# Another order of the features in the recurrent stage: 512-byte runs for x's second load and the output's stores

## The chip, the cores and the metric

The kernel runs on one core of a Trainium2 chip, as one program. The metric is device time in microseconds (us). Before the change three runs took 1760.66, 1766.8 and 1768.66 us; their median is 1766.8 us. A further execution was taken with the hardware profiler, and took 1754.42 us. All arrays are float32.

## The reference

The input x has 16 batches (B) of 256 time steps (T) with 512 features (D); cond has 16 rows of 512. Two layers follow one another, each added to its input:

```python
# layer 0: attention, its norm scaled and shifted by cond
scale, shift = jnp.split(cond[:, None] @ W_emb + b_emb, 2, axis=-1)
xn = _rms_norm(x, g_norm) * (1.0 + scale) + shift
q, k, v = ...            # xn @ W_qkv, split into 16 heads of 32 features
q, k = _rms_norm(q, g_q), _rms_norm(k, g_k)
attn = softmax(q @ k.T * 32 ** -0.5)
o = attn @ v             # heads joined again to 512 features
x = x + o + o @ W_out

# layer 1: a GRU over the 256 steps, started from h = cond
def cell(h, x):
    i_r, i_z, i_n = jnp.split(x @ W_ih + b_ih, 3, axis=-1)
    h_r, h_z, h_n = jnp.split(h @ W_hh + b_hh, 3, axis=-1)
    r = sigmoid(i_r + h_r); z = sigmoid(i_z + h_z)
    n = tanh(i_n + r * h_n)
    return (1.0 - z) * n + z * h
x = x + scan(cell, cond, x over time)
```

## The kernel before

The core has these engines: TensorE (matmuls, PE in the profile, with its weight loads as PEld), VectorE (DVE), ScalarE (ACT), GpSimd (POOL) and SyncE (SP), which here only issues DMAs. P is 128, the number of partitions; KC is 4, the number of 128-wide pieces of the 512 features.

**Opening and attention.** Batch by batch, load_x brings a batch of x into SBUF with time on the partitions. The norm's statistics are taken on ScalarE (norm_first, L171), the rows are scaled on VectorE (norm_apply, L178), turned by TensorE so that features lie on the partitions (turn_x, L194), then scaled and shifted by cond (put_x). project (L220) multiplies by W_qkv; four matmuls with 32 columns of weights each fill the four 32-column strips of the array. Logits, maxima, exponentials, normalization and the weighted sum follow in four slots per batch (slot0 to slot3), each slot overlapping the attention of one group of heads with the projection of the next batch. The result stays in SBUF as oT, features on partitions. In the opening, batches 0, 1 and 2 go through the first steps with nothing yet to overlap: `load_x(0)`, `load_x(1)`, `load_x(2)` stand among the loads of the weights in SP's queue.

**Recurrent stage.** State, inputs and outputs lie with features on the partitions, 32 features of one "q" of each 128-wide piece per 32-partition strip. x is loaded a second time for it, in blocks of 8 steps (TG), by load_block (L687): eight DMAs of 32 KB per block, one for each strip j and half of the block s. in_blocks gives the access pattern in DRAM. put_block (L733) turns a block on VectorE in 32 x 32 squares. output_step (L719) and put_output add the attention's output projection to it, a group of 16 steps ahead of use. For a step, the gates r, z and n are accumulated in PSUM: the bias (open_gate, L757, for the first two pairs of steps; seed, L769 to L771, after that), the input's part for two steps at once (input_part) and the state's part (state_part), both through gate_part (L775), which puts the state or input on the array as weights of 16 or 32 columns and streams 128 columns of wih or whh past it, once for each of the four strips. VectorE turns the gates in 32 x 32 squares (L799), ScalarE applies sigmoid and tanh, VectorE updates h, and GpSimd adds x (L908). After 8 steps store (L811) turns the block back on VectorE and writes it in eight DMAs of 32 KB. The last block is turned by TensorE and written by store_last.

Which feature sits in which strip is set in four places that have to agree: in_blocks, the columns that gate_part streams, the columns of wo that product and project_first use, and the rows of wih and whh, which must match the features on the partitions. The bias rows b_rows are made from two row loads (L118, L119), a transpose (L628), and in slot2 of batches 1 to 4 a broadcast copy and a 32 x 32 transpose for each row of gates (L476, L479).

**What sets the order.** TensorE, VectorE, ScalarE and GpSimd run their instructions in the order in which the program text issues them. DMAs go to SP's queue (and a few to ScalarE's) in the order of the text, each one waiting for its inputs or for its buffer. A completion semaphore is given to each DMA in turn out of eight, so a DMA also waits until the one eight places before it has landed.

Of the kernel before, what the change touches and what calls it, by code (L numbers as in the profile page):

```python
# [8 lines left out]
F32 = mybir.dt.float32  # L9
# [10 lines left out]
def kernel(  # L20
# [52 lines left out]
    for k in range(KC):  # L73
        nc.scalar.dma_start(cond_sb[k * B : (k + 1) * B, :], cond[:, k * P : (k + 1) * P])
    h0T = const.tile([P, KC, B], F32, name="h0T")

    cols = const.tile([P, 38], F32, name="cols")

# [24 lines left out]

    rows_b = p1.tile([26, P], F32, tag="qkn", name="rows_b", bufs=4)

    wq = wpool.tile([P, KC, 3 * D], F32, tag="w_b", name="wq")
    for i in range(3):
        for k in range(KC):
            nc.sync.dma_start(
                wq[:, k, i * D : (i + 1) * D], w_qkv[k * P : (k + 1) * P, i * D : (i + 1) * D]  # L110
            )
        if i == 0:
            for r, g in ((0, g_q), (1, g_k)):
                nc.sync.dma_start(
                    rows_b[r : r + 1, :].rearrange("o (i d) -> o i d", d=DH),
                    g.rearrange("(o i d) -> o i d", o=1, i=1).to_broadcast([1, HG, DH]),
                )
            nc.sync.dma_start(rows_b[2:14, :], b_ih.rearrange("(m c) -> m c", c=P))  # L118
            nc.sync.dma_start(rows_b[14:26, :], b_hh.rearrange("(m c) -> m c", c=P))  # L119
        if i == 1:  # L120
            load_x(1)


# [3 lines left out]
    qT = p1.tile([P, NG, T], F32, name="qT")  # L127
    kT = p1.tile([P, NG, T], F32, name="kT")


# [316 lines left out]
    def slot2(b, w, prev, st):  # L447
# [19 lines left out]
        if b == 0:  # L467

            for c in range(KC):
                d = wo[:, c, c * P : (c + 1) * P]  # L470
                nc.vector.tensor_tensor(d, d, ident, ALU.add)
        elif b <= 4:
            i = b - 1
            wide = small.tile([P, KC, 32], F32, tag="wide", name=f"wide_{i}", bufs=1)
            c0 = (0, 4, 8, 20)[i]
            nc.vector.tensor_copy(  # L476
                wide, cols[:, 14 + c0 : 18 + c0].unsqueeze(2).to_broadcast([P, KC, 32])
            )
            nc.vector.transpose(b_rows[:, i, :], wide.rearrange("p q b -> p (q b)"))  # L479
        st.accs = (st.q1, k)  # L480
# [34 lines left out]
    def project_first(k):  # L515
        if k == 0:
            first.extend(tile_ps(f"first_{i}", f"lg{i}", (P, 2, TI * B)) for i in range(KC // 2))
        for m in range(KC):
            for j in range(4):
                nc.tensor.matmul(  # L520
                    first[m // 2][32 * j : 32 * j + 32, m % 2, :],
                    wo[:, k, m * P + 32 * j : m * P + 32 * j + 32],
                    oT[:, k, 0:TI, :].rearrange("p t b -> p (t b)"),
# [47 lines left out]
    with tc.manual_schedule(engines=ORDERED):  # L571
# [42 lines left out]
        wih = wpool.tile([P, KC, 3 * D], F32, tag="w_a", name="wih")  # L614
        for k in range(KC):
            nc.sync.dma_start(wih[:, k, :], w_ih[k * P : (k + 1) * P, :])
        tpx = turn_x(0, "AX")
# [9 lines left out]
        tp = tile_ps("tp_rows_b", "lg3")  # L627
        nc.tensor.transpose(tp[:, :26], rows_b, ident[:26, :26])  # L628
        nc.vector.tensor_copy(cols[:, 12:], tp[:, :26])
        bcols = cols[:, 14:38]  # L630

        nc.vector.tensor_tensor(bcols[:, 0:8], bcols[:, 0:8], bcols[:, 12:20], ALU.add)
        nc.vector.tensor_scalar(gq_col, cols[:, 12:13], DH ** -0.5, None, ALU.mult)
# [42 lines left out]
    def in_blocks(a, i, j, s):  # L676

        a = a[:, i * TG : (i + 1) * TG, :].rearrange("b (s i) (q j c) -> s j b i q c", s=2, j=4, c=32)
        return a[s, j]

    def load_block(i):
        if i < T // TG:
            xins[i] = xin.tile([P, TG // 2, KC, 32], F32, tag="xin", name=f"xin_{i}")
            for j in range(4):
                for s in range(2):
                    r = 32 * j + B * s
                    nc.sync.dma_start(xins[i][r : r + B], in_blocks(x, i, j, s))  # L687

# [4 lines left out]
    whh = wpool.tile([P, KC, 3 * D], F32, tag="w_b", name="whh")  # L693
    for k in range(KC):
        nc.sync.dma_start(whh[:, k, :], w_hh[k * P : (k + 1) * P, :])

# [19 lines left out]
    def product(acc, w, m, k, rhs):  # L716

        for j in range(4):
            nc.tensor.matmul(  # L719
                acc[32 * j : 32 * j + 32, :],  # L720
                w[:, k, m * P + 32 * j : m * P + 32 * j + 32],
                rhs,
# [50 lines left out]
    def gate_part(dst, rows, w, g, k, stationary):  # L773
        for j in range(4):
            nc.tensor.matmul(  # L775
                dst[32 * j : 32 * j + rows, :],
                stationary,
                w[:, k, g * D : (g + 1) * D].rearrange("p (q j c) -> p j q c", q=KC, c=32)[:, j],
                start=False,
# [24 lines left out]
    def store(i, y):  # L804
# [3 lines left out]
        for j in range(4):  # L808
            for s in range(2):
                r = 32 * j + B * s  # L810
                nc.sync.dma_start(in_blocks(out, i, j, s), osb[r : r + B])  # L811

    def store_last(y, tl, n):

        tp = tile_ps(f"tpy_{tl}", ("lg1", "lg0")[n == 1], (P, KC, P))
        for q in range(KC):
            nc.tensor.transpose(
                tp[0 : n * B, q, :], y[:, q, tl * B : (tl + n) * B], ident
            )
        ol = gru.tile([P, KC, P], F32, tag="osb", name=f"ol_{tl}")  # L820
        t0 = T - TG + tl
        dst = out[:, t0 : t0 + n, :].rearrange("b t (q c) -> t b q c", c=P)
        if n > 1:
            nc.scalar.copy(ol[0 : n * B], tp[0 : n * B])
            nc.sync.dma_start(dst, ol[0 : n * B])
            return
        for i, (copy, queue) in enumerate(
            ((nc.vector.tensor_copy, nc.sync), (nc.scalar.copy, nc.scalar))
        ):
            q = slice(2 * i, 2 * i + 2)  # L830
            copy(ol[0:B, q], tp[0:B, q])
            queue.dma_start(dst[0, :, q], ol[0:B, q])

    with tc.manual_schedule(engines=ORDERED):
# [11 lines left out]
        for g in (R_, N_, Z_):  # L846
            open_gate(0, g)
            state_part(0, g, h0T)
            for k in range(KC):
                input_part(0, g, k)  # L850
        parts = [(g, k) for g in (R_, N_, Z_) for k in range(KC)]
        hT = h0T
        for t in range(T):
# [102 lines left out]
```

## Time and profile before

| what | us |
|---|---|
| median of three runs | 1766.8 (1760.66 to 1768.66) |
| profiled execution | 1754.42 |
| its span, first to last instruction | 1752.6 |
| TensorE occupied | 1729.9 (99%) |
| weight loads (PEld) | 1355.0 |
| VectorE | 1056.8 |
| ScalarE | 739.5 |
| GpSimd | 315.5 |
| recurrent stage, from the first gate to the end | 626 to 1752.6 |

DMA in the profiled execution: 146266 packets, of which 137899 are smaller than 512 bytes, 44.48 MB in all.

How to read it: the page gives each engine's busy time, then the span in 40 equal slices with the busy share in tenths. The rows of groups give line, engine, operation, output and inputs, shapes, count, then busy time and mean ns of one instruction, then the idle time of the engine before them and what ended it. Matmuls overlap: the mean of one, 273 ns for a gate matmul, is the time from its start to its end, and the rate at which they follow one another is read from the starts in the timeline. An "x2" in the count of matmuls comes from float32, which takes two instructions for each matmul of the text. SPq and ACTq rows are the issuing of DMAs.

### The profile page before, as it was taken

The numbers are of one execution on the slowest core, as the hardware profiler recorded it, in microseconds if no ns is written. First come the engines' busy times: TensorE is split into PE (matmuls) and PEld (weight loads), VectorE is DVE, ScalarE is ACT, GpSimd is POOL, SyncE is SP. The second block draws the span as 40 slices with busy tenths as digits, with TensorE's granted clock in tenths as the row PEclk, the third lists the DMA queues.
The fourth block names the chain that finished last, engine by engine and source line by source line (L and its number), as shares of the span: only waits on it lengthen the run. The fifth ranks groups of instructions, "written<-read, shape, count | busy, mean of one in ns | idle before, by whom it ended". The sixth has DMA issues, their size and how long they took to land.

```text
span 1752.6 us, 103775 instructions
## 1 busy us (share of the span) xinstructions
PE 1729.9 (99%) x46955; PEld 1355.0 (77%) x46955; DVE 1056.8 (60%) x3324; ACT 739.5 (42%) x2690; POOL 315.5 (18%) x773
## 2 busy tenths in 40 slices
PE   7999999999999999999999999999999999999998
PEld 2444444444444589999999999999999999999997
DVE  4777777777776745555555555555555555555554
ACT  3777777777777722222222222222222222222222
POOL 0344443444334410000000000000000000000000
PEclk9999999999999899999999999999999999999999
DMA  8100000000000111101110111011101100000000
GB/s 287 28 14 14 14 27 14 14 14 14 14 2 2 73 28 20 19 17 19 24 19 17 21 23 18 17 21 22 19 17 21 24 17 17 16 11 11 11 16 16
DMA packets 146266, 44.48 MB, mean 25 GB/s; under 512 B 137899, under 2 KB 138031, under 8 KB 145823
## 3 DMA queue, kind: packets, MB, share of 16 engines
q1 hardware_dynamic: 145351, 36.73, 9.2%
q8 instruction: 368, 6.03, 1.4%
q10 hardware_dynamic: 472, 1.10, 0.2%
q14 instruction: 75, 0.61, 0.1%
HBM read 29.41 MB, written 8.39 MB: 22 GB/s over the span
## 4 chain that ended last, share of the span: by engine, by line
PE 96%; DVE 2%; ACT 1%; DMA 1%; issue 0%; DVEq 0%; ACTq 0%
PE qkv L220 19%; PE gn L775 19%; PE gr L775 19%; PE gz L775 19%; PE o L719 6%; PE lg L285 4%; PE tpa L194 4%; PE o L364 4%; PE tpqk L194 1%; ACT attn L307 1%; PE tpx L194 1%; PE first L520 0%; DMA x<-in_x_dram 0%; DMA we<-in_L_cond_W_emb_dram 0%; DVE trh L799 0%
## 5 line engine op out<-in xcount | busy, mean ns | idle before, releaser
L220 PE MATMUL qkv<-wq,xnT 128*32 128x512 f32 x3072 | 357.6, 600 | 0.6 <-DVE xnT L212 0.6
L318 POOL TENSOR_SCALAR attn<-attn,rden 128x256 f32<-128x256 f32 x510 | 232.8, 478 | 383.1 <-DVE rden L315 262.9
L873 ACT ACTIVATE r<-trr 128x64 f32<-128x64 f32 x256 | 65.4, 256 | 515.6 <-DVE trr L799 515.6
L307 ACT ACTIVATE attn<-lg,neg 128x256 f32<-128x256 f32 x512 | 234.4, 483 | 67.8 <-DVE neg L301 45.1
L799 DVE STREAM_TRANSPOSE trr<-gr 128x128 f32<-128x128 f32 x256 | 81.1, 317 | 247.5 <-PE gr L775 247.4
L220 PEld LDWEIGHTS qkv<-wq,xnT 128*32 128x32 f32 x3072 | 87.6, 110 | 183.4 <-issue 158.9
L877 ACT ACTIVATE n<-n 128x64 f32<-128x64 f32 x256 | 65.7, 257 | 309.8 <-DVE n L876 306.8
L301 DVE TENSOR_REDUCE neg<-lg 128x2 f32<-128x512 f32 x256 | 159.2, 684 | 50.4 <-PE lg L285 50.4
L799 DVE STREAM_TRANSPOSE trh<-gn 128x128 f32<-128x128 f32 x256 | 81.1, 317 | 142.2 <-PE gn L775 142.2
L775 PE MATMUL gn<-wih,xT 128*32 128x128 f32 x4096 | 159.7, 273 | 0.0
L719 PE MATMUL o<-oT,wo 128*32 128x256 f32 x1920 | 148.0, 379 | 0.0
L775 PE MATMUL gr<-whh,padded 128*32 128x128 f32 x4096 | 135.9, 273 | 2.3 <-DVE padded L906 1.4
L908 POOL TENSOR_TENSOR y<-xT,padded 128x64 f32<-128x64 f32 x128 | 41.0, 321 | 533.5 <-DVE padded L906 533.5
L775 PE MATMUL gr<-wih,xT 128*32 128x128 f32 x4096 | 136.1, 273 | 0.0
L775 PEld LDWEIGHTS gn<-wih,xT 128*32 128x32 f32 x4096 | 120.4, 110 | 20.3
L775 PE MATMUL gz<-wih,xT 128*32 128x128 f32 x4096 | 136.0, 273 | 0.0
L775 PE MATMUL gz<-whh,padded 128*32 128x128 f32 x4096 | 135.8, 273 | 0.0
L775 PE MATMUL gn<-whh,padded 128*32 128x128 f32 x4096 | 135.7, 273 | 0.0
L775 PE MATMUL gr<-whh,h 128*16 128x128 f32 x4064 | 134.6, 273 | 0.3
L775 PE MATMUL gz<-whh,h 128*16 128x128 f32 x4064 | 134.2, 273 | 0.2
L775 PE MATMUL gn<-whh,h 128*16 128x128 f32 x4064 | 134.2, 273 | 0.0
L775 PEld LDWEIGHTS gr<-wih,xT 128*32 128x32 f32 x4096 | 117.4, 110 | 20.5
(122 smaller groups left out, 2731.4 us busy)
## 6 DMA issues: line engine op xcount, KB each, us to landing
x<-in_x_dram SPq DMA_DIRECT2D x16, 512.0 KB, 4.0
xin<-in_x_dram SPq DMA_DIRECT2D x256, 32.0 KB, 2.5
out_dram<-osb SPq DMA_DIRECT2D x248, 32.0 KB, 1.9
wq<-in_L_cond_W_qkv_dram SPq DMA_DIRECT2D x12, 256.0 KB, 4.8
wih<-in_L_cond_W_ih_dram SPq DMA_DIRECT2D x4, 768.0 KB
whh<-in_L_cond_W_hh_dram SPq DMA_DIRECT2D x4, 768.0 KB
we<-in_L_cond_W_emb_dram SPq DMA_DIRECT2D x2, 512.0 KB, 4.8
we<-in_L_cond_W_emb_dram ACTq DMA_DIRECT2D x2, 512.0 KB
```

Of the source, the lines that this page charges most:

```text
L194: nc.tensor.transpose(dst[r], src[q], ident[q, q])
L220: nc.tensor.matmul(a[32 * j : 32 * j + 32, :], batches[b].xnT[:, k, n * P + 32 * j : n * P + 32 * j + 32], wq[:, k, s * D : (s + 1) * D], ...
L285: nc.tensor.matmul(w.lg[i][:, n, :], qT[r, g, n * P : (n + 1) * P], kT[r, g, :], start=True, stop=True,)
L301: nc.vector.tensor_reduce(w.neg[:, i, :], w.lg[i], AX.X, ALU.max, negate=True)
L307: nc.scalar.activation(a[:, n, :], w.lg[i][:, n, :], AF.Exp, bias=w.neg[:, i, n : n + 1], accum_out=w.den[:, i, n : n + 1],)
L318: engine.tensor_scalar(w.attn[i][:, n, :], w.attn[i][:, n, :], w.rden[:, i, n : n + 1], 1.0, ALU.mult, ALU.mult,)
L364: nc.tensor.matmul(w.o[i * DH : (i + 1) * DH, :], v[:, k, h * DH : (h + 1) * DH], w.attnT[:, i, k, :], start=(k == 0), stop=(k == NT - 1),)
L719: nc.tensor.matmul(acc[32 * j : 32 * j + 32, :], w[:, k, m * P + 32 * j : m * P + 32 * j + 32], rhs, start=(k == 0), stop=(k == KC - 1),)
L775: nc.tensor.matmul(dst[32 * j : 32 * j + rows, :], stationary, w[:, k, g * D : (g + 1) * D].rearrange("p (q j c) -> p j q c", q=KC, c=32)[ ...
L799: nc.vector.transpose(tr.rearrange("p q s b -> p (q s b)"), gate)
L873: nc.scalar.activation(r, turned("r", t, gr[:, 0, :])[:, :, s, :], AF.Sigmoid)
L877: nc.scalar.activation(n, n, AF.Tanh)
```

## The change

The features get another place. Before, partition 32j + c of piece q held feature 128q + 32j + c; after, it holds feature 128j + 32q + c. So the 128 features of one strip j lie side by side in DRAM, and the runs that load_block reads and store writes have 128 elements (512 bytes) in place of 32 (128 bytes). The rest follows from that:

- gate_part streams 128 adjacent columns in place of four runs of 32; product and project_first take other columns of wo.
- wih and whh have their rows in the new order, so each is loaded by load_rows in 16 DMAs of 32 partitions instead of 4 of 128.
- the start state in the new order, h0P, is made from cond by four more loads (cond_p) and one more transpose. h0T stays, for the attention's scale and shift.
- the bias rows are loaded already broadcast, by 12 DMAs after the last loads of W_qkv; slot2 of batch 1 adds the two biases of r and z, and the four copies and transposes in slot2 go.
- store_last reads PSUM in the permuted order when it copies.

```diff
--- before.py
+++ after.py
@@ -73,8 +73,9 @@
     for k in range(KC):
         nc.scalar.dma_start(cond_sb[k * B : (k + 1) * B, :], cond[:, k * P : (k + 1) * P])
     h0T = const.tile([P, KC, B], F32, name="h0T")
-
-    cols = const.tile([P, 38], F32, name="cols")
+    h0P = const.tile([P, KC, B], F32, name="h0P")
+
+    cols = const.tile([P, 14], F32, name="cols")
 
     work = ctx.enter_context(ExitStack())
     p1 = work.enter_context(tc.tile_pool(name="p1", bufs=1))
@@ -101,7 +102,9 @@
 
     load_x(0)
 
-    rows_b = p1.tile([26, P], F32, tag="qkn", name="rows_b", bufs=4)
+    rows_b = p1.tile([2, P], F32, tag="qkn", name="rows_b", bufs=4)
+    cond_p = p1.tile([KC * B, P], F32, tag="qkn", name="cond_p", bufs=4)
+    b_more = p1.tile([P, 2, P], F32, name="b_more")
 
     wq = wpool.tile([P, KC, 3 * D], F32, tag="w_b", name="wq")
     for i in range(3):
@@ -115,10 +118,22 @@
                     rows_b[r : r + 1, :].rearrange("o (i d) -> o i d", d=DH),
                     g.rearrange("(o i d) -> o i d", o=1, i=1).to_broadcast([1, HG, DH]),
                 )
-            nc.sync.dma_start(rows_b[2:14, :], b_ih.rearrange("(m c) -> m c", c=P))
-            nc.sync.dma_start(rows_b[14:26, :], b_hh.rearrange("(m c) -> m c", c=P))
+            for k in range(KC):
+                nc.sync.dma_start(
+                    cond_p[k * B : (k + 1) * B, :].rearrange("b (j c) -> b j c", c=32),
+                    cond.rearrange("b (j k c) -> k b j c", k=KC, c=32)[k],
+                )
         if i == 1:
             load_x(1)
+    for j in range(4):
+        bi, bh = (
+            b.rearrange("(o g j f) -> j o g f", o=1, g=3, f=P)[j].to_broadcast([32, 3, P])
+            for b in (b_ih, b_hh)
+        )
+        r = slice(32 * j, 32 * j + 32)
+        nc.sync.dma_start(b_rows[r, 0:3, :], bi)
+        nc.sync.dma_start(b_rows[r, 3, :], bh[:, 2, :])
+        nc.sync.dma_start(b_more[r], bh[:, 0:2, :])
 
 
 
@@ -126,6 +141,13 @@
 
     qT = p1.tile([P, NG, T], F32, name="qT")
     kT = p1.tile([P, NG, T], F32, name="kT")
+
+    def load_rows(dst, w):
+
+        for k in range(KC):
+            for j in range(4):
+                r = P * j + 32 * k
+                nc.sync.dma_start(dst[32 * j : 32 * j + 32, k, :], w[r : r + 32, :])
 
 
     def tile_ps(name, bank, shape=(P, D)):
@@ -469,14 +491,8 @@
             for c in range(KC):
                 d = wo[:, c, c * P : (c + 1) * P]
                 nc.vector.tensor_tensor(d, d, ident, ALU.add)
-        elif b <= 4:
-            i = b - 1
-            wide = small.tile([P, KC, 32], F32, tag="wide", name=f"wide_{i}", bufs=1)
-            c0 = (0, 4, 8, 20)[i]
-            nc.vector.tensor_copy(
-                wide, cols[:, 14 + c0 : 18 + c0].unsqueeze(2).to_broadcast([P, KC, 32])
-            )
-            nc.vector.transpose(b_rows[:, i, :], wide.rearrange("p q b -> p (q b)"))
+        elif b == 1:
+            nc.vector.tensor_tensor(b_rows[:, 0:2, :], b_rows[:, 0:2, :], b_more, ALU.add)
         st.accs = (st.q1, k)
         st.rstd = st.s1.rs.second()
         normalize(w)
@@ -519,7 +535,7 @@
             for j in range(4):
                 nc.tensor.matmul(
                     first[m // 2][32 * j : 32 * j + 32, m % 2, :],
-                    wo[:, k, m * P + 32 * j : m * P + 32 * j + 32],
+                    wo[:, k, P * j + 32 * m : P * j + 32 * m + 32],
                     oT[:, k, 0:TI, :].rearrange("p t b -> p (t b)"),
 
                     start=(k == 0 and m % 2 == 0),
@@ -612,8 +628,7 @@
         nc.sync.dma_start(wo, w_out.rearrange("(k p) n -> p k n", p=P))
 
         wih = wpool.tile([P, KC, 3 * D], F32, tag="w_a", name="wih")
-        for k in range(KC):
-            nc.sync.dma_start(wih[:, k, :], w_ih[k * P : (k + 1) * P, :])
+        load_rows(wih, w_ih)
         tpx = turn_x(0, "AX")
         for c in range(KC):
             put_x(0, 0, tpx, (c,))
@@ -625,11 +640,10 @@
         k = project(0, 0, 1, range(KC), "Z")
         tpx = turn_x(1, ("lg0", "lg1"))
         tp = tile_ps("tp_rows_b", "lg3")
-        nc.tensor.transpose(tp[:, :26], rows_b, ident[:26, :26])
-        nc.vector.tensor_copy(cols[:, 12:], tp[:, :26])
-        bcols = cols[:, 14:38]
-
-        nc.vector.tensor_tensor(bcols[:, 0:8], bcols[:, 0:8], bcols[:, 12:20], ALU.add)
+        nc.tensor.transpose(tp[:, :2], rows_b, ident[:2, :2])
+        nc.tensor.transpose(tp[:, 64 : 64 + KC * B], cond_p, ident[: KC * B, : KC * B])
+        nc.vector.tensor_copy(cols[:, 12:], tp[:, :2])
+        nc.vector.tensor_copy(h0P.rearrange("p k b -> p (k b)"), tp[:, 64 : 64 + KC * B])
         nc.vector.tensor_scalar(gq_col, cols[:, 12:13], DH ** -0.5, None, ALU.mult)
         nc.vector.tensor_copy(gk_col, cols[:, 13:14])
         s0 = Stats(0, 0)
@@ -675,7 +689,7 @@
 
     def in_blocks(a, i, j, s):
 
-        a = a[:, i * TG : (i + 1) * TG, :].rearrange("b (s i) (q j c) -> s j b i q c", s=2, j=4, c=32)
+        a = a[:, i * TG : (i + 1) * TG, :].rearrange("b (s i) (j f) -> s j b i f", s=2, f=P)
         return a[s, j]
 
     def load_block(i):
@@ -684,15 +698,16 @@
             for j in range(4):
                 for s in range(2):
                     r = 32 * j + B * s
-                    nc.sync.dma_start(xins[i][r : r + B], in_blocks(x, i, j, s))
+                    nc.sync.dma_start(
+                        xins[i][r : r + B].rearrange("b i q c -> b i (q c)"), in_blocks(x, i, j, s)
+                    )
 
     for i in range(4):
         load_block(i)
 
 
     whh = wpool.tile([P, KC, 3 * D], F32, tag="w_b", name="whh")
-    for k in range(KC):
-        nc.sync.dma_start(whh[:, k, :], w_hh[k * P : (k + 1) * P, :])
+    load_rows(whh, w_hh)
 
     work.close()
 
@@ -718,7 +733,7 @@
         for j in range(4):
             nc.tensor.matmul(
                 acc[32 * j : 32 * j + 32, :],
-                w[:, k, m * P + 32 * j : m * P + 32 * j + 32],
+                w[:, k, P * j + 32 * m : P * j + 32 * m + 32],
                 rhs,
                 start=(k == 0),
                 stop=(k == KC - 1),
@@ -775,7 +790,7 @@
             nc.tensor.matmul(
                 dst[32 * j : 32 * j + rows, :],
                 stationary,
-                w[:, k, g * D : (g + 1) * D].rearrange("p (q j c) -> p j q c", q=KC, c=32)[:, j],
+                w[:, k, g * D + P * j : g * D + P * j + P],
                 start=False,
                 stop=True,
                 skip_group_check=True,
@@ -808,7 +823,9 @@
         for j in range(4):
             for s in range(2):
                 r = 32 * j + B * s
-                nc.sync.dma_start(in_blocks(out, i, j, s), osb[r : r + B])
+                nc.sync.dma_start(
+                    in_blocks(out, i, j, s), osb[r : r + B].rearrange("b i q c -> b i (q c)")
+                )
 
     def store_last(y, tl, n):
 
@@ -817,19 +834,20 @@
             nc.tensor.transpose(
                 tp[0 : n * B, q, :], y[:, q, tl * B : (tl + n) * B], ident
             )
-        ol = gru.tile([P, KC, P], F32, tag="osb", name=f"ol_{tl}")
+        ol = gru.tile([P, 4, KC, 32], F32, tag="osb", name=f"ol_{tl}")
         t0 = T - TG + tl
-        dst = out[:, t0 : t0 + n, :].rearrange("b t (q c) -> t b q c", c=P)
+        dst = out[:, t0 : t0 + n, :].rearrange("b t (j f) -> t b j f", f=P)
+        src = tp.rearrange("p q (j c) -> p j q c", c=32)
         if n > 1:
-            nc.scalar.copy(ol[0 : n * B], tp[0 : n * B])
-            nc.sync.dma_start(dst, ol[0 : n * B])
+            nc.scalar.copy(ol[0 : n * B], src[0 : n * B])
+            nc.sync.dma_start(dst, ol[0 : n * B].rearrange("p j q c -> p j (q c)"))
             return
         for i, (copy, queue) in enumerate(
             ((nc.vector.tensor_copy, nc.sync), (nc.scalar.copy, nc.scalar))
         ):
-            q = slice(2 * i, 2 * i + 2)
-            copy(ol[0:B, q], tp[0:B, q])
-            queue.dma_start(dst[0, :, q], ol[0:B, q])
+            j = slice(2 * i, 2 * i + 2)
+            copy(ol[0:B, j], src[0:B, j])
+            queue.dma_start(dst[0, :, j], ol[0:B, j].rearrange("p j q c -> p j (q c)"))
 
     with tc.manual_schedule(engines=ORDERED):
         padded = []
@@ -845,11 +863,11 @@
                 nc.vector.tensor_tensor(a, o[:, :, c], a, ALU.add)
         for g in (R_, N_, Z_):
             open_gate(0, g)
-            state_part(0, g, h0T)
+            state_part(0, g, h0P)
             for k in range(KC):
                 input_part(0, g, k)
         parts = [(g, k) for g in (R_, N_, Z_) for k in range(KC)]
-        hT = h0T
+        hT = h0P
         for t in range(T):
             tl = t % TG
             p, s = divmod(t, 2)
```

## The prediction

> **What bounds the kernel now.** I read the page's busy row first, then the slices, then the busy times by stretch.
>
> ```profile
> PE 1729.9 (99%) x46955; PEld 1355.0 (77%) x46955; DVE 1056.8 (60%) x3324; ACT 739.5 (42%) x2690; POOL 315.5 (18%) x773
> ...
> DMA  8100000000000111101110111011101100000000
> ...
> q1 hardware_dynamic: 145351, 36.73, 9.2%
> ```
>
> TensorE is occupied for 1729.9 of 1752.6 us, so all its idle time is 22.7 us; the DMA engines are busy only in the first slice of 43.8 us. A change to transfers can save no more than the part of those 22.7 us that a transfer causes. Where they lie, by stretch (columns: the stretch and its length, then busy us of PE, PEld, DVE, ACT, POOL, granted clock, DMA share, GB/s):
>
> ```profile
> 0.00:44.00 44.00, 32.98 (x319) 11.81 (x323) 19.11 (x62) 16.31 (x45) 0.70 (x6) 1.00 0.81 286
> ...
> 88.00:600.00 512.00, 510.81 (x6872) 239.35 (x6866) 375.14 (x851) 394.91 (x1338) 207.54 (x455) 1.00 0.06 19
> ...
> 626.00:1735.00 1109.00, 1107.62 (x38547) 1060.13 (x38540) 607.38 (x2275) 278.99 (x1138) 81.00 (x253) 1.00 0.10 18
> ```
>
> In the recurrent stage, where all the altered loads of x and stores of the output run, TensorE is idle for 1.4 of 1109 us, and the waits of that stage name VectorE and never a DMA. Eleven us of idle time lie in the opening, before the DMAs have delivered the first inputs. Whether "busy" is really full speed is read from the matmul starts (columns: start us, length us, then the group):
>
> ```profile
> 1400.33 1.06 PE L775 MATMUL gr<-whh,h 128*16 128x128 f32 x32
> 1401.20 1.06 PE L775 MATMUL gn<-whh,h 128*16 128x128 f32 x32
> 1402.08 1.06 PE L775 MATMUL gz<-whh,h 128*16 128x128 f32 x32
> 1402.95 0.61 PE L719 MATMUL o<-oT,wo 128*32 128x256 f32 x8
> 1403.38 1.06 PE L775 MATMUL gr<-wih,xT 128*32 128x128 f32 x32
> ```
>
> Start to start, 96 gate instructions take 1402.95 - 1400.33 = 2.62 us: 27.3 ns each, or 109.2 ns for four in the four column strips. The projection (L719) takes 0.43 us for 8: 53.8 ns each, for 256 columns.
>
> **The change, part by part.**
>
> *1. The moving weights of the gates (L775).* 128 columns in four runs of 32, 512 bytes apart, become one run of 128. There are 3 x (4096 + 4096 + 4064 + 32) = 36,864 such instructions, so 0.1 ns on each is 3.7 us; this is the only edit with a large multiplier. Rows with contiguous moving operands are near: L719 at 53.8 ns for 256 columns, and L220 at 107.25 ns for 512 (groups of 72 and of 32 on the critical chain last 7.86 and 3.57 us: 4.29 us over 40). A line through these two gives 0.209 ns a column and 27.0 ns for 128, against 27.3 now. So an excess of 0.3 ns could be due to the runs, which would be 0.3 x 36,864 = 11 us. But L719's start-to-start is read from only 8 instructions at a resolution of 0.01 us, plus or minus 1 ns. The Trainium skill (TensorE: Matmul & The Clock Gate, "Wait — 56ns, not 53.3ns?") gives warm matmuls N / 2.4 GHz plus a fixed 2.5 ns whatever N is. With two clocks a column, which 4 x 107.25 = 429 ns for 512 columns shows (1024 clocks are 426.7), 128 columns should cost 106.7 + 2.5 = 109.2 ns for four, just what the strided gates take now. By the row's line the gain is 11 us, by the rule 0. I take 0: the open-gate matmuls (L757), whose moving operand b_rows is contiguous and has 128 columns, have the gates' own mean of 273 ns, and 16 of them start within 0.44 us, 27.5 ns each. Bounds: -11 to 0; a loss is excluded, as contiguous rows are nowhere slower.
>
> *2. Loads of xin (256) and output stores (248).* The same number of DMAs of the same 32 KB, each with 64 runs of 512 bytes instead of 256 of 128. They already land in 2.5 and 1.9 us against blocks that live 8 steps, some 35 us. Nobody waits: 0. Hidden by 4.4 us of matmuls a step; without that cover it would be a landing of about 2 us per block. The packet count falls by 504 x 192 = 96,768, so 146,266 goes to about 50,000.
>
> *3. SP's queue in the opening.* Here work is added. Each new DMA reuses the completion semaphore of the one eight before it, so SP also waits for landings. What stands there now:
>
> ```profile
> 12.24 2.17 SPq L109 DMA_DIRECT2D wq<-in_L_cond_W_qkv_dram  x4
> 14.45 0.43 SPq L99 DMA_DIRECT2D x<-in_x_dram  x1
> ...
> 18.09 0.38 SPq L99 DMA_DIRECT2D x<-in_x_dram  x1
> ...
> 20.56 0.63 ACT L171 ACTIVATE xs<-x 128x512 f32<-128x512 f32 x1 [2.98 <-DMA x<-in_x_dram]
> ...
> 30.07 0.61 ACT L171 ACTIVATE xs<-x 128x512 f32<-128x512 f32 x1
> ```
>
> First, four cond_p loads replace the two bias-row loads (0.35 us each). At 0.35 to 0.55 us each (bias rows, wq) the second third of wq starts 1.2 us later, and x_1 about 1.5 us later, at 16.0. ScalarE waits for x_1 until 20.56, so its statistics slip to about 22.1; x_1's scaled copy on VectorE, now done at 24.0, is done at 25.5, and TensorE turns it at 26.05. Hidden with 0.5 us to spare: 0, up to 1.5. The wq part is wanted only at about 22 us, some 3 us after it lands.
>
> Next, twelve broadcast bias loads (393 KB) come ahead of x_2, wo, wih, x_3, x_4 and xin. The fourth shares a semaphore with x_1 and can't issue before x_1 lands, near 22.0; the fifth to eighth follow the landings of the last wq parts (to about 24.3); four more at 0.4 to 0.5 us each put x_2's issue at about 26.3, against 18.09. Loads of x land in 3.4 to 8.0 us in this stretch; with the queue short I take 4.0: x_2 arrives at 30.3, where ScalarE now begins on it at 30.07 without a wait. Behind it on ScalarE stands a square of q, which VectorE could take 0.5 us later than now; then the scaling of x_2 and TensorE's turning of it at 34.6, which already waits 0.16 us. So lateness beyond 0.5 us is paid one for one by TensorE. Bounds: 0, if the twelve cost 0.35 us each, to 3.5, at the 0.77 us of the dearest small row (L114) with a landing in 4.5; I take 0.5.
>
> *4. wih and whh in 16 DMAs of 32 partitions instead of 4 of 128.* A rule speaks against this: the Trainium skill (SBUF — State Buffer, "Door 1: The DMA port swizzle") says that 32 partitions reach only half of the ports, measured at 189 GB/s. Now, whh:
>
> ```profile
> 591.00:594.00 3.00, 2.39 (x39) 1.73 (x36) 2.93 (x5) 2.22 (x10) 1.14 (x3) 1.00 0.95 395
> 594.00:597.00 3.00, 2.78 (x13) 1.59 (x14) 1.06 (x5) 2.57 (x10) 2.67 (x6) 0.67 1.02 422
> 597.00:600.00 3.00, 3.00 (x26) 1.08 (x27) 1.56 (x3) 1.93 (x8) 0.98 (x3) 0.50 0.49 198
> ```
>
> At the rate of the rows, about 410 GB/s, 3.15 MB take 7.7 us; at the rule's they take 16.6 us (an estimate) and end near 608. The first use of whh is at 626.0, so both are hidden. For wih, the queue behind it counts: with wo and wih moving from 27 us, x_3 would arrive near 50 by the rule (near 40 by the row), and ScalarE reads it first at 57.15. Cost 0.
>
> *5. Small edits.* One more transpose (cond_p) on TensorE, beside L628's 0.17 us to the next start: +0.1. VectorE loses four copies (220 ns) and four transposes (312 ns) of the bias and gains one add of 256 columns (417 ns at L751, the nearest row): 1.7 us off an engine with 137 us free in 88 to 600 us, where TensorE idles 1.2 in all: 0. In the last step the copies read PSUM in runs of 32; L347's scattered copy costs 606 ns on ScalarE and L240's plain one 608: 0, within 0.3 either way.
>
> Sum: 0 + 0 + 0.5 + 0 + 0.1 = +0.6 us on the profiled execution's 1754.4 us (span 1752.6 and 1.8 around it): 1755.0. The median of the runs is 1766.8, 12.4 us above that execution; the same addition gives 1767.4.
>
> **Rivals.**
>
> *A. Contiguous weights speed up TensorE.* For it: the 0.3 ns by the line of the two contiguous lengths, and that nothing else limits the stage. Against it: L757's 27.5 ns. It would give 1767 - 11 = 1756 us, or 1761 with half.
>
> *B. Slower, through x_2.* Place: the twelve bias loads ahead of it on SP; price: 1 us of TensorE per us of x_2 beyond 30.6. TensorE's instructions begin at half speed in this stretch (at 16.55 us, 0.85 us for 8 of L220, later 0.43), so a pause may cost as much again. With 3.5 us for x_2 and 1.5 for x_1 it gives 1767 + 5 = 1772. To be slower by 0.5% (8.8 us, about what a measurement of this kernel can tell from no change), x_2 must land after 39.4, that is in 13 us at my issue time; the longest landing seen for x is 8.0.
>
> *C. The runs don't get longer,* because the packets stay at 128 bytes: the packet count would stay near 146,000. The time would be 1767 all the same, since part 2 is worth nothing.
>
> **How the numbers follow.** Likeliest, no visible change: 0.81 (C included at 0.02). A: 0.09, of which half reaches 0.5%. B: 0.10, of which half passes 0.5% (a stall that I have not sized, or a clock that stays low after it). Runs of one kernel spread from 1760.66 to 1768.66, so I leave 0.02 more on either side for that alone: faster 0.06, slower 0.07, same 0.87. The prediction is 1767. The range goes from A's full gain, 1756, to B's 1772 plus 4 us, half of that spread: 1776.
>
> **What would show it.** Right: packets near 50,000 and a lower share of q1; gate instructions at 27.3 ns; about 1.4 us idle on TensorE in the recurrent stage; the third L171 pair on ScalarE at 30 to 31.5 us, with a wait for x of at most 1.5; whh landed well before the first gate. Wrong: gate starts under 27.1 ns (A), a wait for x of many us in the first 44 (B), or TensorE idle before its first use of whh.

## The result, and the profile after

The changed kernel takes 1773.16 us in the median (1769.76 to 1779.63), the kernel before 1768.8 us in the same comparison: a ratio of 1.0031 with a 95% interval of 1.0017 to 1.0046. It is slower by 0.3%, some 5 us, less than the 0.5% below which the prediction counted a difference as none. Measured a second time, in another comparison, the ratio was 1.0012 (0.9994 to 1.0031). So the loss is a few microseconds, and its size is known to no better than about plus or minus 2 us.

The profiled execution of the changed kernel took 1777.96 us (span 1776.2). The page's busy row, its DMA slices and the row of the queue that the change is about:

```profile
PE 1746.6 (98%) x46956; PEld 1379.9 (78%) x46956; DVE 1055.7 (59%) x3317; ACT 740.2 (42%) x2690; POOL 316.9 (18%) x773
...
DMA  8200000000000310000000010000000000000000
...
q1 hardware_dynamic: 50199, 37.15, 8.2%
```

The packets of q1 fell from 145351 to 50199: the change does what it says, and the queue's share went from 9.2% to 8.2%. The DMA slices of the recurrent stage, a mixture of 0 and 1 before, are now nearly all 0. TensorE did not get shorter by it. Busy times by stretch, as in the prediction (stretch and length, then busy us of PE, PEld, DVE, ACT, POOL, granted clock, DMA share, GB/s):

```profile
0.00:44.00 44.00, 31.30 (x288) 10.98 (x289) 17.29 (x58) 15.11 (x40) 0.70 (x6) 0.88 0.81 243
88.00:600.00 512.00, 510.69 (x6888) 239.51 (x6880) 375.25 (x849) 393.90 (x1331) 208.26 (x455) 1.00 0.06 16
626.00:1735.00 1109.00, 1103.20 (x37804) 1065.60 (x37799) 596.29 (x2230) 272.96 (x1112) 79.76 (x249) 1.00 0.08 18
```

Three things are to be seen. In the first 44 us TensorE did 288 matmuls where it had done 319, and its granted clock is 0.88. Two thirds of what is missing there lie from 13.9 to 20.7 us, ahead of x_2, and are not the change's: the profile of before has no record of the clock ahead of 21.6 us (the view prints 1.00 for it), but its 64 products from 16.55 us on took 9.57 us, the 64 of the changed kernel from 16.01 took 9.38, and 64 at full clock take 7.07 in both. The other third follows on x_2 and is shown below. The attention stage is as it was. In the recurrent stretch TensorE started 743 matmuls fewer; at 27.2 ns each that is some 20 us, of which 2.8 us are only the later start of the stage (its first gate starts at 628.73 where it was 625.88). The other 17 us look like the change's doing. They are not: the first experiment below shows them in the kernel before as well.

The opening, queue of SP first (start us, length us, then the group of DMA issues):

```profile
16.02 0.43 SPq L100 DMA_DIRECT2D x<-in_x_dram  x1
...
21.96 0.31 SPq L134 DMA_DIRECT2D b_rows<-in_L_cond_b_ih_dram  x1
...
25.53 0.32 SPq L135 DMA_DIRECT2D b_rows<-in_L_cond_b_hh_dram  x1
...
27.30 0.42 SPq L136 DMA_DIRECT2D b_more<-in_L_cond_b_hh_dram  x1
27.86 0.39 SPq L100 DMA_DIRECT2D x<-in_x_dram  x1
```

x_1 is issued at 16.02, the fourth bias load waits until 21.96, the last of the twelve goes out at 27.30, and x_2 at 27.86, where it had gone out at 18.09. What ScalarE and TensorE make of that (the bracket is the idle time ahead of the group and what ended it):

```profile
21.97 0.63 ACT L193 ACTIVATE xs<-x 128x512 f32<-128x512 f32 x1 [4.93 <-DMA x<-in_x_dram]
...
31.75 0.63 ACT L193 ACTIVATE xs<-x 128x512 f32<-128x512 f32 x1 [2.23 <-DMA x<-in_x_dram]
```

```profile
33.42 0.71 PE L216 MATMUL tpqk<-ident,qkn 64*128 64x64 f32 x16
35.90 1.04 PE L216 MATMUL tpx<-ident,xs 64*128 64x64 f32 x16 [1.76 <-DVE xs L200]
36.87 5.34 PE L242 MATMUL qkv<-wq,xnT 128*32 128x512 f32 x32
...
43.91 1.15 PE L307 MATMUL lg<-kT,qT 32*128 32x256 f32 x16
```

In the kernel before the same rows were:

```profile
33.87 0.71 PE L194 MATMUL tpqk<-ident,qkn 64*128 64x64 f32 x16
34.61 1.04 PE L194 MATMUL tpx<-ident,xs 64*128 64x64 f32 x16
35.58 3.64 PE L220 MATMUL qkv<-wq,xnT 128*32 128x512 f32 x32
...
40.93 1.15 PE L285 MATMUL lg<-kT,qT 32*128 32x256 f32 x16
```

ScalarE waits 2.23 us for x_2, TensorE 1.76 us for its scaled rows; and the 32 products behind the pause take 5.34 us where they took 3.64. The granted clock of the changed kernel by stretch says why:

```profile
34.00:37.00 3.00, 1.12 (x26) 0.78 (x24) 2.69 (x9) 0.87 (x3) 0.00 (x0) 1.00 1.09 234
37.00:42.00 5.00, 5.00 (x32) 1.15 (x28) 2.60 (x8) 1.15 (x4) 0.00 (x0) 0.66 1.02 221
42.00:45.00 3.00, 2.94 (x47) 1.52 (x43) 0.88 (x2) 1.43 (x3) 0.00 (x0) 1.00 1.02 224
```

A mean of 0.66 over 5 us is half clock for 3.4 of them: the clock falls about 2 us after the pause has ended, and comes back. As a measure for all that follows I take the time from the end of the transposes of q and k (tpqk) ahead of x_2's to the first logits (lg). In the kernel before it is 40.93 - 34.58 = 6.35 us; here it is 43.91 - 34.13 = 9.78. The difference of 3.4 us is 1.7 us of longer wait (from the start of tpqk to that of tpx it is 2.48 us instead of 0.74) and 1.7 us of half clock. The logits of the attention stage then keep their distance from the first ones to within 0.2 us for 549 us in both kernels, so the opening's delay is not made good on the way. The last batch and the handing over to the recurrent stage vary more: from the first logits to the first gate it is 585.0 us in the first profile of before and 583.4 in its second, 584.8 and 582.0 in the two of the changed kernel.

### The profile page after: what moved, and what is told of

Same layout as the page of the kernel before. It is cut to its first block, busy times and chain, and to the rows that moved or that the text cites. A ratio compares the mean times of both kernels' runs of the same rounds, so it can differ in the third digit from the quotient of the medians.

```text
span 1776.2 us, 103821 instructions
## 1 busy us (share of the span) xinstructions
PE 1746.6 (98%) x46956; PEld 1379.9 (78%) x46956; DVE 1055.7 (59%) x3317; ACT 740.2 (42%) x2690; POOL 316.9 (18%) x773
## 2 busy tenths in 40 slices
DMA packets 51114, 44.90 MB, mean 25 GB/s; under 512 B 9747, under 2 KB 42879, under 8 KB 50671
## 3 DMA queue, kind: packets, MB, share of 16 engines
q1 hardware_dynamic: 50199, 37.15, 8.2%
## 4 chain that ended last, share of the span: by engine, by line
PE 96%; DVE 1%; ACT 1%; DMA 1%; issue 1%; DVEq 0%; ACTq 0%
PE gr L790 19%; PE qkv L242 19%; PE gn L790 19%; PE gz L790 18%; PE o L734 6%; PE lg L307 4%; PE tpa L216 4%; PE o L386 4%; PE tpqk L216 1%; ACT attn L329 1%; DMA x<-in_x_dram 1%; PE tpx L216 1%; PE first L536 0%; DMA we<-in_L_cond_W_emb_dram 0%; DVE trh L814 0%
## 5 line engine op out<-in xcount | busy, mean ns | idle before, releaser
L790 PE MATMUL gn<-wih,xT 128*32 128x128 f32 x4096 | 190.8, 273 | 0.7 <-issue 0.2
L734 PE MATMUL o<-oT,wo 128*32 128x256 f32 x1920 | 178.0, 379 | 0.3
L790 PEld LDWEIGHTS gn<-wih,xT 128*32 128x32 f32 x4096 | 153.4, 110 | 10.2 <-issue 2.4
L790 PE MATMUL gz<-whh,h 128*16 128x128 f32 x4064 | 151.5, 273 | 1.4 <-issue 1.0
L790 PE MATMUL gz<-wih,xT 128*32 128x128 f32 x4096 | 152.3, 273 | 0.3
L790 PE MATMUL gr<-wih,xT 128*32 128x128 f32 x4096 | 151.3, 273 | 0.4
L790 PE MATMUL gr<-whh,h 128*16 128x128 f32 x4064 | 150.1, 273 | 0.7
L790 PE MATMUL gz<-whh,padded 128*32 128x128 f32 x4096 | 150.2, 273 | 0.4 <-issue 0.2
L790 PE MATMUL gn<-whh,h 128*16 128x128 f32 x4064 | 150.0, 273 | 0.3
L790 PEld LDWEIGHTS gr<-wih,xT 128*32 128x32 f32 x4096 | 135.3, 110 | 10.8 <-issue 1.6
```

What stands on the lines that cost most here:

```text
L734: nc.tensor.matmul(acc[32 * j : 32 * j + 32, :], w[:, k, P * j + 32 * m : P * j + 32 * m + 32], rhs, start=(k == 0), stop=(k == KC - 1),)
L790: nc.tensor.matmul(dst[32 * j : 32 * j + rows, :], stationary, w[:, k, g * D + P * j : g * D + P * j + P], start=False, stop=True, skip_gr ...
```

## The experiments

All ratios are to the kernel before, measured in the same comparison. The first four ran together, then the next four, then the last two.

**e1_before_again: the kernel before, unchanged.** No edit.

> The kernel before, unchanged. Theory 1 (the opening alone carries the loss): its time equals that of before within 0.15%, and its recurrent stage, from the first open-gate matmul to the last gate of the last step, lasts 1117 us as in the first profile, so that the 1137 us of the changed kernel's profile is the change's doing. Theory 2 (short pauses of TensorE in the recurrent stage, put down to issue, come and go in either kernel): the stage's length lies anywhere from 1117 to 1137 us, with 10 us or more above 1117 in most profiles, because 1754 us was below every timed run of before.

Measured 1.0007 (0.9995 to 1.002). The recurrent stretch of its profile, and TensorE's waits in it (engine, line, what it waited for: total us, times, longest us):

```profile
626.00:1735.00 1109.00, 1103.86 (x38010) 1036.95 (x38004) 599.07 (x2247) 276.03 (x1126) 79.99 (x250) 1.00 0.10 18
```

```profile
PEld gz L775 <- issue: 7.4, 21, 0.6
PEld gn L775 <- issue: 5.0, 14, 0.6
...
PEld gr L775 <- issue: 2.5, 9, 0.4
```

The same view of the profile that the prediction rests on has only these rows of the kind:

```profile
PEld gz L775 <- issue: 0.9, 3, 0.4
...
PEld o L719 <- issue: 0.2, 1, 0.2
```

With the row of L719, which is 0.2 us in e1 too, the unchanged kernel shows 15.1 us of pauses that the profile puts down to issue (the engine waits for nothing that the profile shows), against 1.1 us in its first profile; the changed kernel's two profiles have 17.2 and 10.9 us. From the first gate to the first transpose of the last output it is 1119.5 us in that first profile of before and 1135.2 us here; all the other profiles of this study lie between 1131.4 and 1140.1, the two of the changed kernel (1140.1 and 1134.1) among them. The first profile, at 1754.42 us faster than each of the three timed runs of before, was a lucky one, and the 17 us between the two recurrent stages are no effect of the change.

**e3_gate_columns: contiguous moving weights alone**, on the kernel before.

```
-                w[:, k, g * D : (g + 1) * D].rearrange("p (q j c) -> p j q c", q=KC, c=32)[:, j],
+                w[:, k, g * D + P * j : g * D + P * j + P],
```

> The kernel before with one edit: the gates stream 128 adjacent columns of the weights, the wrong ones for its layout, so the gates are computed from other features; the work is the same in amount. If the four runs of 32 columns cost nothing (prediction): 27.3 ns from start to start and a ratio of 1.000, within 0.0015. If they cost 0.3 ns an instruction: 0.994. If adjacent columns disturb the stream (a loss that I had excluded): above 1.002.

Measured 1.0008 (0.9993 to 1.0023), with 1135.8 us for the recurrent stage against 1135.2 in the unchanged kernel. One run of 128 columns is worth nothing that can be seen against four runs of 32: the 36,864 gate matmuls neither gain nor lose.

**e4_bias_loads_only and e10_bias_loads_again: the kernel before with the twelve bias loads, and nothing else of the change**, in the place that they have in the changed kernel. What they load is used by nothing.

```
+    b_more = p1.tile([P, 2, P], F32, name="b_more")
 ...
+    for j in range(4):
+        bi, bh = (
+            b.rearrange("(o g j f) -> j o g f", o=1, g=3, f=P)[j].to_broadcast([32, 3, P])
+            for b in (b_ih, b_hh)
+        )
+        r = slice(32 * j, 32 * j + 32)
+        nc.sync.dma_start(b_rows[r, 0:3, :], bi)
+        nc.sync.dma_start(b_rows[r, 3, :], bh[:, 2, :])
+        nc.sync.dma_start(b_more[r], bh[:, 0:2, :])
```

> The kernel before with the twelve broadcast bias loads added ahead of x_2 and not used (b_rows is written again later, as before). Theory 1: x_2 is late by 1 to 2 us, TensorE turns it 1 to 1.5 us later and runs the next projection at half clock for 2 us, so the time is 2.5 to 4 us more than before, a ratio of 1.0015 to 1.0025. If the opening is not the cause, within 0.5 us of before.

> The kernel before with the twelve bias loads ahead of x_2, a second time. Its first profile showed a wait of TensorE for x_2 of 0.24 us only, worth 0.2 us, and yet its ratio was 1.0022. If x_2 lands at the edge, a little later in most executions than in that profile: a wait of 0.5 us or more and perhaps the 32 products at half clock (5.3 us), and ratio 1.001 to 1.002. If the profile was typical: wait about 0.2 us, ratio 1.000, and the first measurement lay at the edge of its spread.

Measured 1.0022 (1.001 to 1.0034), and the second time 1.0014 (1.0003 to 1.0026). The two profiles differ. In the first, x_2 came 0.52 us late for ScalarE and TensorE waited 0.24 us, with no fall of the clock (6.56 us by the measure above). In the second, TensorE's rows are those of the changed kernel:

```profile
31.14 0.72 PE L205 MATMUL tpqk<-ident,qkn 64*128 64x64 f32 x16
33.66 1.09 PE L205 MATMUL tpx<-ident,xs 64*128 64x64 f32 x16 [1.80 <-DVE xs L189]
34.68 5.23 PE L231 MATMUL qkv<-wq,xnT 128*32 128x512 f32 x32
...
41.61 1.15 PE L296 MATMUL lg<-kT,qT 32*128 32x256 f32 x16
```

The same wait and the same half clock: 41.61 - 31.86 = 9.75 us. So the twelve loads alone can bring the whole of the opening's loss. Whether they do in an execution is not set by x_2 alone: ScalarE took it at 29.52 us in the second profile, earlier than in the first (30.40), but TensorE came to it earlier still, with the transposes ahead of it done at 31.86 us against 34.30. In the first profile TensorE's products ran at half clock until 20.5 us, in the second the full clock is on record from 17.5 us on. With these loads x_2 lies at the edge, and the slower the opening's first part, the more of its lateness is hidden.

**e2_bias_late and e8_bias_and_cond_late: the changed kernel without them in that place.** In e2 the twelve loads are taken from their place ahead of x_2 and stand behind wih, ahead of x_3; in e8 the four loads of cond_p stand behind x_1 as well.

```
     load_rows(wih, w_ih)
+        for j in range(4):
+            ...
+            nc.sync.dma_start(b_rows[r, 0:3, :], bi)
+            nc.sync.dma_start(b_rows[r, 3, :], bh[:, 2, :])
+            nc.sync.dma_start(b_more[r], bh[:, 0:2, :])
```

> The changed kernel with the twelve bias loads moved behind wih on SP, ahead of x_3. If the late x_2 and the half clock after it carry the loss (theory 1): ScalarE takes x_2 without a wait near 30 us, the first logits are back at about 41 us from 43.9, and the time is 3 us less than the changed kernel's, 1.0013 to 1.002 of before. If the recurrent stage carries it (theory 2 with more pauses after the change): the first logits are back at 41 us as well, but the time stays within 1 us of 1.003.

> The changed kernel with the twelve bias loads behind wih (as in the run that moved them alone) and the four loads of cond_p behind x_1 as well. If x_1 is hidden, as the prediction's part 3 has it: x_1 is taken at about 21.2 us in place of 21.9, and nothing else moves: ratio 1.000, as with the bias loads moved alone. If x_1's 0.8 us were paid: about 0.8 us less, ratio 0.9995; against the run with the bias loads alone that is at the edge of what can be told, and the start of the first transposes of x_1 and of the first logits in the profile decides.

Measured 1.0003 (0.9988 to 1.0018) and 1.0006 (0.9987 to 1.0024): the loss is no longer seen, with everything else of the change in its place. TensorE of e2:

```profile
33.53 0.71 PE L207 MATMUL tpqk<-ident,qkn 64*128 64x64 f32 x16
34.09 1.04 PE L207 MATMUL tpx<-ident,xs 64*128 64x64 f32 x16
35.06 3.64 PE L233 MATMUL qkv<-wq,xnT 128*32 128x512 f32 x32
...
40.40 1.15 PE L298 MATMUL lg<-kT,qT 32*128 32x256 f32 x16
```

No wait, full clock, 6.16 us by the measure; e8 has 6.16 too. x_1, taken at 21.92 in e2, was taken at about 19 us in e8, and the first logits stand at 40.40 and 40.23: x_1's later arrival is hidden, as the prediction had it. That holds for openings like these. In the quicker ones of the kernel before TensorE did wait for x_1's scaled rows, 1.44 us in e1 and 0.31 us in e3; there a later x_1 would be paid for, but none of the five profiles with the loads of cond_p shows such an opening.

**e5_bias_loads_double: 24 loads in place of 12**, as in e4, each load of two or three rows cut into loads of one.

```
-        nc.sync.dma_start(b_rows[r, 0:3, :], bi)
+        for g in range(3):
+            nc.sync.dma_start(b_rows[r, g, :], bi[:, g, :])
         nc.sync.dma_start(b_rows[r, 3, :], bh[:, 2, :])
-        nc.sync.dma_start(b_more[r], bh[:, 0:2, :])
+        for g in range(2):
+            nc.sync.dma_start(b_more[r, g, :], bh[:, g, :])
```

> The kernel before with the bias loads of the changed kernel ahead of x_2, as in the run with the twelve loads alone, but each of three or two rows is cut into loads of one row: 24 loads in place of 12; what they load is used by nothing. Theory 1 (x_2's lateness sets the loss): twelve more issues of about 0.45 us on SP move x_2's issue from 26.6 to about 32 us, its landing from 30.4 to about 36 us, the third pair of transposes of x from 34.5 to about 40 us, and the first logits from 40.9 to 46 to 48 us (48 where the products after the pause run at half clock). Ratio to the kernel before 1.005 to 1.0065. Theory 2 (the loss of the run with twelve loads lies elsewhere, and the opening's lateness is made good later): ratio 1.002 as with twelve.

Measured 1.0039 (1.0024 to 1.0055).

```profile
35.76 0.63 ACT L184 ACTIVATE xs<-x 128x512 f32<-128x512 f32 x1 [5.61 <-DMA x<-in_x_dram]
```

```profile
39.90 1.41 PE L207 MATMUL tpx<-ident,xs 64*128 64x64 f32 x16 [5.33 <-DVE xs L191]
41.23 5.44 PE L233 MATMUL qkv<-wq,xnT 128*32 128x512 f32 x32
...
48.37 1.15 PE L298 MATMUL lg<-kT,qT 32*128 32x256 f32 x16
```

x_2 was taken at 35.76 us, where 36 was expected, TensorE's wait grew to 5.33 us, and the first logits stand at 48.37. By the measure it is 13.81 us, 7.5 more than before; the timed loss is 0.0039 of 1769.6, 6.9 us (4.2 to 9.7). The ratio came out lower than expected, perhaps because the expectation added the new delay to the first ratio of e4, which the second measurement of it put lower. The price is that of theory 1: 5.3 us of longer wait for an x_2 taken 5.7 us later than before, and half clock once.

**e6_after_again: the changed kernel a second time.** No edit.

> The changed kernel, unchanged, a second time, for a second profile. If the half clock after the wait for x_2 belongs to the wait: the 32 products behind the third pair of transposes of x take about 5.3 us again (3.64 at full clock) and the first logits stand at about 43.9 us. If it was an accident of that execution: 3.64 us, and first logits at about 42.2 us. Ratio to the kernel before 1.003 in both.

Measured 1.0012 (0.9994 to 1.0031).

```profile
36.62 1.04 PE L216 MATMUL tpx<-ident,xs 64*128 64x64 f32 x16 [1.84 <-DVE xs L200]
37.59 5.34 PE L242 MATMUL qkv<-wq,xnT 128*32 128x512 f32 x32
...
44.63 1.15 PE L307 MATMUL lg<-kT,qT 32*128 32x256 f32 x16
```

The half clock is there again after a wait of 1.84 us, with 9.85 us by the measure. It belongs to the wait, and is no accident of one execution.

**e7_weights_by_32_rows: wih and whh in sixteen transfers each**, on the kernel before, every row to its old place.

```
-        for k in range(KC):
-            nc.sync.dma_start(wih[:, k, :], w_ih[k * P : (k + 1) * P, :])
+        for k in range(KC):
+            for j in range(4):
+                r = P * k + 32 * j
+                nc.sync.dma_start(wih[32 * j : 32 * j + 32, k, :], w_ih[r : r + 32, :])
```

(whh in the same way, by a function of both.)

> The kernel before with wih and whh each loaded in sixteen transfers of 32 rows in place of four of 128, every row to the place it had. The prediction's part 4 (hidden): x_3 issued near 45 us in place of 33, taken with no longer wait than before; whh landed before the first gate; ratio 1.000, within 0.9985 to 1.0015. Rival (a transfer of 32 partitions is slow enough to be seen, or x_3 comes late): ratio 1.002 or more, with a wait of ScalarE for x_3 or of TensorE for whh.

Measured 0.9988 (0.9969 to 1.0007): nothing lost. The busy times while whh is on its way (the last two columns are the DMA engines' share and GB/s):

```profile
591.00:595.00 4.00, 3.40 (x15) 1.89 (x16) 2.22 (x6) 3.81 (x16) 2.44 (x6) 0.77 1.01 230
595.00:599.00 4.00, 4.00 (x45) 2.08 (x41) 2.38 (x5) 1.93 (x8) 1.23 (x3) 0.50 1.03 230
```

With 32 partitions to a transfer the engines are fully busy at 230 GB/s, where before 395 and 422 GB/s were moved by engines as busy. whh is all there by about 602 us, more than 20 us ahead of the first gate. x_3 went out at 35.66 us rather than 45, and was taken at 55.42 without a wait.

**e9_values_before_x2: work for TensorE during the wait.** On the changed kernel two neighbours are exchanged:

```
-        st.tpx = turn_x(2, "YZ")
         v = project(0, 0, 2, range(KC), "lg2")
+        st.tpx = turn_x(2, "YZ")
```

> The changed kernel with two neighbours on TensorE exchanged: the products of the values of batch 0 (32 of 128x512, 3.64 us at full clock) stand ahead of the transposes of x_2 in place of behind them, so that TensorE has work while x_2's rows are on their way. SP's queue, and with it the bias loads ahead of x_2, stays as it is. Theory 1 (the whole loss is TensorE's wait for x_2, 1.8 us, and the half clock that follows it, 1.7 us): x_2 is taken at about 32 us with a wait of ScalarE of about 2.2 us as before, TensorE shows no wait for xs there, the 32 products take 3.64 us, from the end of the transposes tpqk to the first logits it is 6.3 to 6.6 us (before 6.4, changed kernel 9.8), and the ratio to the kernel before is 1.000 (0.9985 to 1.0015). Theory 2 (the lateness of x_2 reaches TensorE another way, or the loss lies in another part): ratio 1.002 to 1.003 as in the changed kernel.

Measured 1.0016 (1.0005 to 1.0028): neither theory as it was written. TensorE, then VectorE:

```profile
33.23 3.64 PE L242 MATMUL qkv<-wq,xnT 128*32 128x512 f32 x32
36.80 0.71 PE L216 MATMUL tpx<-ident,xs 64*128 64x64 f32 x16
39.03 0.97 PE L216 MATMUL tpqk<-ident,qkn 64*128 64x64 f32 x16 [1.52 <-DVE qkn L268]
```

```profile
32.91 0.17 DVE L168 TENSOR_SCALAR m_x<-ssx 128x2 f32<-128x2 f32 x1 [1.48 <-ACT xs L193]
33.96 0.69 DVE L257 TENSOR_REDUCE ssqk<-sq 128x16 f32<-128x512 f32 x1 [0.88 <-ACT sq L253]
```

The wait for xs is gone and the 32 products run at full speed, as theory 1 said. But a new wait of 1.52 us, for qkn, stands ahead of the transposes tpqk that follow x_2's. ScalarE's square of q stands behind its squares of x_2, and VectorE stops 1.48 us for x_2's statistics and 0.88 us for that square; so x_2's lateness also comes to TensorE by the other road, through two engines that work in order. By the measure it is 41.06 - 33.30 = 7.76 us: of the 3.4 us, 2.0 were recovered and 1.4 were left. The timed ratio can't tell 1.4 us from nothing or from the whole.

No version beats the kernel before: e2, with the whole change but the place of the twelve loads, is level with the kernel before.

## Why the prediction was right, and which term was mis-sized

The forecast of no visible change, 1767 us with 1756 to 1776, held: 1773.16 us, 5.5 us of loss by the ratio, under the bound of 0.5%. The places where the change costs nothing were right; the one place where it costs was right too, but its cost was taken too low. Point by point:

*1, the moving weights: right.* Gate instructions in the profile after: from 1400.81 to 1403.42 for 96 of them, 27.2 ns each, where 27.3 was said. e3, with that edit alone, shows no gain and no loss. Of the row's 11 us and the rule's 0 the rule was right; rival A falls.

*2, the loads of xin and the stores: right.* The packets came to 51114 where about 50,000 was said, and nobody waits for these transfers in the stage. Rival C falls: the runs did get longer.

*3, SP's queue: the right place, mis-sized.* The first half holds to within 0.2 us: x_1 issued at 16.02 (16.0 said), taken at 21.97 (22.1), and hidden. In the second half the fourth bias load went at 21.96 (22.0), but the fifth to eighth, which were to follow the landings of wq until about 24.3, went until 25.53. x_2 was issued at 27.86 instead of 26.3; it landed 3.9 us later (4.0 said), so it was taken at 31.75 where 30.3 was taken as likeliest. That is outside the 30 to 31.5 us, with a wait of 2.23 us where at most 1.5 was to show no harm. The second mis-sizing is the price. "Paid one for one" leaves out the clock: 1.7 us of added wait brought 1.7 us of half clock. The term of 0.5 us measured 3.4 us, just inside its bounds of 0 to 3.5. Rival B had both the place and this price ("a pause may cost as much again"); at its 1772 us it gave the time better than the likeliest case did, though part of that is chance: its 1.5 us for x_1 did not show, and the kernel before measured 1768.8 beside it, not 1766.8.

*4, wih and whh by 32 rows: right, by way of the rule.* whh's transfers moved at 221 to 237 GB/s in e7 and in the changed kernel, somewhat above the 189 of the Trainium skill (SBUF — State Buffer, "Door 1: The DMA port swizzle") and far from the 410 of the row. In the changed kernel the last of them is issued by 601.4 and lands 5.6 us later, at about 607 (608 by the rule), over 20 us ahead of the first gate at 628.73. x_3, issued at 45.4 (loads of x land in 3.7 us in the median, so near 50, as the rule had it), is taken at 60.11 without a wait. e7 shows the part to be free.

*5, small edits: nothing seen.* The two transposes stand 0.35 us ahead of the next product in the profile after, where the one stood 0.17 ahead: 0.2 us more, 0.1 was said. VectorE's and ScalarE's edits show nowhere.

*What was said to show it, and didn't:* 1.4 us of idle time on TensorE in the recurrent stage. There are 5.8 us, and 5.1 in the unchanged kernel's second profile. The figure was read from one execution, whose recurrent stage was some 12 us or more shorter than in every later profile. The prediction did set the 12.4 us between that execution and the median aside, and added its sum to the median; had it been held to the profile's own time, the result would have looked like a loss of over 20 us.

What stays open: the sum of the opening, 3.4 us, is within the intervals of both measurements of the changed kernel (5.5 and 2.1 us), and e2, e4, e5 and e10 put it there; a further effect of a microsecond or two elsewhere would not have been seen. One place for it is the opening ahead of the measure. The first logits stood at 40.93, 38.73, 38.61 and 39.21 us in the four profiles with the bias loads of before (the first, e1, e3, e7), at 40.40 and 40.23 in e2 and e8, and at 43.91 and 44.63 in the changed kernel: the opening of one kernel varies by some 2 us, and whether the change adds a little to it beside x_2's 3.4 us these few profiles can't tell.

## What to carry to other kernels

A load whose consumer has half a microsecond to spare is priced by what is put ahead of it in its queue: count every issue, and every landing that an issue waits for, and take the late end of each. Where it may make TensorE stop, allow for a fall of the clock beside the wait; here that doubled the price. A small load that nobody needs soon goes behind the ones that somebody waits for; here moving twelve of them back cost nothing that was seen and gave back the opening's 3.4 us. Profile the unchanged kernel twice before a single profile's idle time is believed.

## What the runs showed of the hardware

A wait of TensorE of less than 2 us can be followed by half clock. After waits of 1.76, 1.84 and 1.80 us for x_2 (the changed kernel twice, and e10) the granted clock fell to 0.50, 1 to 2 us after the wait had ended, for about 3.4 us, and cost 1.6 to 1.7 us each time; after e5's 5.33 us it fell too; after waits of 0.24 us (e4) and of 1.52 us (e9) it did not. What counts as idle for the clock these runs leave open, since transposes stand on both sides of each wait. From the start of the first transposes behind the last products to the start of the next products 3.45, 3.52 and 3.54 us passed in those three profiles with a fall (7.38 in e5), and 1.94 and 3.14 us in the two without. The Trainium skill (TensorE: Matmul & The Clock Gate, "Part 1: The HAM clock gate") gives one idle window of about 3.4 us as what brings the half clock. If transposes don't count as work, all six cases agree with it; if they do, half of it was enough. No run here separates the two.

In the recurrent stage TensorE's weight loads pause for up to 0.6 us at a time with nothing that the profile shows to wait for, 44 times and 14.9 us in e1's three rows above, though in the first profile of the same kernel only four times and 1.1 us. The stage has one matmul every 27 ns, so its instructions come in fast, and fetching them is a candidate; no run here tests it, and the cause is open.
